# A selective-scan network on one core: two sums over states made a step later, their bank copied behind a decay, and two tiles for squares

## The chip, the core and the metric

The kernel runs on one core of a Trainium2 chip. The metric is the device time of one execution in microseconds (us). Engines are named as in the profile: PE (TensorE, matmuls), DVE (VectorE), ACT (ScalarE), POOL (GpSimd), SP (the queue that issues the DMAs).

## The reference, cut to what matters

Four images of 64 x 64 pixels and 96 channels pass four layers. Layer 0 normalises by groups, projects to 192 channels, convolves, and runs a selective scan along the rows and along the columns of the image, each of them forwards and backwards; then a depthwise and pointwise convolution (layer 1), attention without softmax and a quantised feed-forward network (layer 2), and a filter in the Fourier domain and a second feed-forward network (layer 3). The scan is the core of it:

```
def step(h, inp):
    u_t, dt_t, B_t, C_t = inp
    dA = jnp.exp(dt_t[..., None] * A)
    h = dA * h + (dt_t * u_t)[..., None] * B_t[:, None, :]
    y = jnp.sum(h * C_t[:, None, :], axis=-1)
    return (h, y)
...
def _ln_t(v, eps=1e-5):
    m = jnp.mean(v, axis=-1, keepdims=True)
    s = jnp.var(v, axis=-1, keepdims=True)
    return (v - m) / jnp.sqrt(s + eps)
```

There are 4 images x 2 orientations x 192 channels x 16 states x 4096 positions, each scanned in both directions. `y` is the sum over the 16 states of the state `h` times `C`.

## The kernel before, in words

A group is 8 channels with 16 states each, 128 rows, in one image and one orientation: N = 192 groups, numbered n. A group's 4096 positions are four chunks q = 0 to 3 of 1024. The loop over n (L1712) has eight steps a group, written out by hand: four forward (L1716, q rising) and four backward (L1764, k = 0 to 3, q falling). The order in which instructions are issued in the text is the order in each engine's queue.

In a step DVE runs one scan (L1741 forward, into a tile S; L1792 backward, in place in the decay's PSUM tile) and, backward, adds the result to S (L1802). From group 54 or so, when the other images' inputs have been made ("pre" in `done`), the last backward scan is left apart in a tile dl and not added. ACT computes the decays `pa` (`decay`, L1495), a step ahead, into two PSUM tiles of two banks each that take turns; so a decay waits for the scan that frees its tile. POOL multiplies by B before the scan (`times_b`, L1478) and by C after it (`times_c`, L1482, and `times_c_apart`, L1487). PE sums over states (`reduce`, L1509): a chunk is two matmuls with `red`, each into 32 rows of one PSUM bank, `py`; the profile counts a matmul of f32 as two instructions. Two chunks fill the bank, half 1 (chunks 3 and 2) or half 0 (chunks 1 and 0); `result` (L1517) copies the bank out to `ys` on ACT, and `store_result` issues four stores on SP. There is one bank `py`, so the next half's first sum waits for the copy of the last.

Before the change the order is, for group n:

- backward k = 1, 2, 3: products with C of chunks 3, 2, 1;
- backward k = 3: sums of chunks 3 and 2 (half 1);
- forward q = 0 of group n+1, at the end of the step: copy of half 1; the decay of chunk 2 comes next on ACT;
- q = 1: product of chunk 0 and sum of chunk 1; q = 2: the apart product, and the store of half 1;
- backward k = 0 of group n+1: sum of chunk 0; k = 2: copy of half 0; k = 3: its store.

There are five S tiles (`place_of`). Group n+1's scans of chunks 1, 2 and 3 write the tiles that held group n's S of chunks 3, 2 and 1, so each waits until that chunk has been summed.

Around these steps `pieces(step)` (called once a step) issues side work in small portions: the projections, convolutions and gates of images 1 to 3 (until about group 54), the turns of scanned data, and layers 1 to 3 of images 0 to 2. Each portion has a planned cost per engine (PE, ACT, POOL, DVE, DMA), and a portion is issued when the step's credit for the engines (`gains`, `short_gains`) allows it. `yield NEXT` puts the rest off to the next step; `clock[0]` counts steps. Side work has three PSUM banks (`bank_taker`); `held` is a list of evictions that wait their turn, with the step from which they count, and `settle` makes those with a cost on ACT wait one step more in the steps where ACT is short (residues 7, 0, 1).

Two pieces of side work are touched. Layer 1 (`layer1`) makes nine matmuls (L861) a block of 512 pixels and evicts them on ACT (`finish`, L833). The normalisation (`layernorm`) takes, for each block, a matmul that centres it (L905), two ACT instructions that copy it out (L894) and square it (L897), and a matmul that sums the squares into `p_var` (L887); it is split in two halves of four blocks. While the scan runs (`deep` = 1) a half has one tile for squares, so the square of a block waits for the variance matmul of the block before.

The part after the scan (from 5401 us) ends the side work and does image 3's layers 1 to 3 with all engines.

Of the kernel before, what the change touches and what calls it, by code (L numbers as in the profile page):

```python
# [19 lines left out]
HW = 64  # L20
L = HW * HW
C = 96
# [51 lines left out]
def layers(ctx: ExitStack, tc: tile.TileContext, a: dict, out):  # L74
# [137 lines left out]
    def settle(held):  # L212


        while held:
            cost, f, args, since = held[0]
            if cost[1]:
                while ordered[0] and clock[0] == since and (clock[0] - 1) % 8 in (7, 0, 1):
                    yield NEXT
            yield cost  # L220
            held.pop(0)
            f(*args)
# [580 lines left out]
    def rest(b, take, deep, x1t=None, held=None):  # L803
# [9 lines left out]
        def layer1(wk):  # L813
            x3 = (x1[b] if x1t is None else x1t).rearrange("p (r w) -> p r w", w=HW)

            def load(i):
                r0, lo, hi = rows_of(i)
                if x1t is not None:
                    return x3[:, lo:hi, :], clock[0]
                x = wk.tile([C, RPB + 2, HW], F32, tag="x", name="x", bufs=2)  # L820
                nc.sync.dma_start(x[:, : hi - lo, :], x3[:, lo:hi, :])
                return x, clock[0]

            def arrived(i):
                return done.get(("x1", b), 0) >= min(i + 2, NBLK)

            yield from until(lambda: arrived(0))
            nxt = load(0)
            yield NEXT
            held = []  # L830

            def finish(i, p, give):
                nc.scalar.activation(  # L833
                    t[:, blk(i)], p, AF.Identity, scale=l1s[:, 0:1], bias=l1s[:, 1:2]
                )
                give()
                ready["t1"] = i + 1

            for i in range(NBLK):
                r0, lo, hi = rows_of(i)  # L840
                if nxt is None:
                    yield NEXT
                    yield from settle(held)
                    yield from until(lambda: arrived(i))
                    nxt = load(i)
                    yield NEXT
                (x, since), nxt = nxt, None
                if clock[0] < since + LANDING:
                    yield NEXT
                    yield from settle(held)  # L850
                    yield from steps_past(since, LANDING)
                p, give = yield from take("p_l1", C, held=held)
                p3 = p.rearrange("p (r w) -> p r w", w=HW)
                for k, (ky, kx) in enumerate(conv_taps()):
                    if k % 3 == 0:
                        yield (2.4, 0, 0, 0, 0 if k else 1)
                        if nxt is None and i + 1 < NBLK and arrived(i + 1):
                            nxt = load(i + 1)
                    dy, dx, ra, rb, ca_, cb_ = tap_window(ky, kx, r0)
                    at = r0 + dy - lo  # L860
                    nc.tensor.matmul(  # L861
                        p3[:, ra:rb, ca_:cb_], lhsT=taps[:, ky * 3 + kx, :],
                        rhs=x[:, at + ra : at + rb, ca_ + dx : cb_ + dx],
                        start=(k == 0), stop=(k == 8),
                    )
                    if k == 2:
                        yield from settle(held)
                held.append(((0, 0.68, 0, 0), finish, (i, p, give), clock[0]))
            yield NEXT
            yield from settle(held)  # L870

        def layernorm(wk, hold, dst, source, result, previous=None):
# [3 lines left out]
            def half_of(h):  # L876
# [12 lines left out]
                def centred(i, pm, give):  # L889
                    if squares and deep == 1:  # L890
                        variance()
                    sq = wk.tile([C, BLK], F32, tag=f"sq{h}", name="sq", bufs=1 if deep == 1 else 4)
                    if ordered[0]:
                        nc.scalar.copy(hold[:, blk(i)], pm)  # L894
                    else:
                        nc.vector.tensor_copy(hold[:, blk(i)], pm)
                    nc.scalar.activation(sq, pm, AF.Square)  # L897
                    give()
                    squares.append((i, sq))
# [575 lines left out]
    def times_b(n, q):  # L1475

        if n < N:
            nc.gpsimd.tensor_tensor(Bs[n, q], Bs[n, q], reps[n // NG, 0, q], ALU.mult)  # L1478
# [19 lines left out]
    def reduce(n, half, chunks=(0, 1)):  # L1498

        if n < 0:  # L1500
            return
        if (n, half) not in pys:
            pys[n, half] = ps.tile([128, BLK], F32, tag="py", name="py")
        py = pys[n, half]
        for j in (2 * c + k for c in chunks for k in range(2)):
            q, k = 2 * half + j // 2, j % 2
            terms = [Ss[n, q]] + ([dls[n, 0]] if q == 0 and n in apart else [])
            for i, x in enumerate(terms):
                nc.tensor.matmul(  # L1509
                    py[32 * j : 32 * j + 32, :], lhsT=red, rhs=x[:, k * BLK : (k + 1) * BLK],  # L1510
                    start=(i == 0), stop=(i == len(terms) - 1),
                )
# [196 lines left out]
    with tc.manual_schedule():  # L1709
        ordered[0] = True  # L1710
        pas = [decay(0, 0, True), None, None, None]
        for n in range(N + 1):  # L1712
# [3 lines left out]
            for q in range(NCH):  # L1716

                if q < 2:
                    load_du(n + 1, q + 2)
                else:  # L1720
                    load_delta(n + 1, q - 2)
                if n % NG == 0 and 0 < n < N and q > 0:
                    load_rep(h, 1, 4 - q)
                if q < 3:
                    pas[q + 1] = decay(n, q + 1, q == 1)
                if q == 0:
                    times_b(n, 3)
                elif q == 1:
                    times_c(n - 1, 0)
                    reduce(n - 1, 0, (1,))  # L1730
                elif q == 2:
                    times_c_apart(n - 1)
                    store_result(n - 1, 1)
                else:
                    times_b(n + 1, 0)
                if end:
                    if q == 0:
                        result(n - 1, 1)
                    continue
                s = Ss[n, q] = big.tile([128, CH], F32, tag=f"S{place_of(n, q)}", name="S")  # L1740
                nc.vector.tensor_tensor_scan(  # L1741
                    s, pas[q], Bs[n, q], Ss[n, q - 1][:, CH - 1 : CH] if q else 0.0,
                    ALU.mult, ALU.add,
                )
                pieces(q)
                if q == 0:
                    result(n - 1, 1)
            if end:
                reduce(n - 1, 0, (0,))
                result(n - 1, 0)  # L1750
# [13 lines left out]
            for k, q in enumerate(reversed(range(NCH))):  # L1764
                if k < 2:
                    times_b(n + 1, k + 1)
                if k > 0:
                    times_c(n, q + 1)
                if k == 0:
                    reduce(n - 1, 0, (0,))  # L1770
                elif k == 1:
                    load_du(n + 2, 0)
                    load_delta(n + 1, 2)
                elif k == 2:
                    load_delta(n + 1, 3)
                else:
                    store_result(n - 1, 0)
                    load_du(n + 2, 1)
                if n % NG == NG - 2:
                    load_rep(h + 1, 0, k)  # L1780
                if k == 1:
                    pas[1] = decay(n, 1, False)
                elif k == 2:
                    pas[0] = decay(n, 0, True)
                    result(n - 1, 0)
                elif k == 3:
                    first = decay(n + 1, 0, True)


                alone = k == 3 and "pre" in done  # L1790
                to = dls[n, 0] if alone else pas[q]
                nc.vector.tensor_tensor_scan(  # L1792
                    to[:, ::-1], pas[q][:, ::-1], Bs[n, q][:, ::-1],
                    edge if k else 0.0, ALU.mult, ALU.add,
                )
                if k < 3:
                    edge = big.tile([128, 1], F32, tag="edge", name="edge", bufs=2)
                    nc.vector.tensor_copy(edge, to[:, 0:1])
                if alone:
                    apart.add(n)  # L1800
                else:
                    nc.vector.tensor_tensor(Ss[n, q], Ss[n, q], to, ALU.add)  # L1802
                if k == 3:
                    reduce(n, 1)
                pieces(4 + k)
                if n == N - 1:
                    for i in (2 * k, 2 * k + 1):
                        last_loads(last_place, i)
# [129 lines left out]
```

## Time and profile before

| what | value |
|---|---|
| median of the runs (3) | 5851.89 us (5849.64 to 5853.17) |
| the profiled execution's own time | 5842.19 us |
| its span | 5840.4 us |
| mean granted PE clock | 0.775 |
| first and last scan | 347 and about 5400 us |

The page gives each engine's busy time with its share of the span, and for each line of the kernel the number of instructions, their busy time, the mean of one in ns, and how long the engine was idle just before them, with what ended most of that. In "A <- B" the first is the instruction that waited, the second what released it.

### The profile page before, as it was taken

What the parts mean: (1) busy time and instruction counts of PE and PEld (TensorE: products, weight loads), DVE (VectorE), ACT (ScalarE), POOL (GpSimd) and SP (SyncE); (2) the same over time, 40 slices, a digit from 0 to 9 for tenths busy, and PEclk for the clock granted to TensorE, in tenths of its full rate; (3) what the DMA queues carried; (4) which work ended last, traced back from release to release, by engine and by line L of the source; (5) the groups of instructions that cost most, each with busy time, mean ns of one, the idle gap of its engine ahead of it and who ended that gap; (6) DMA issues with size and microseconds to landing.
All of it is one profiled execution on the core that took longest, in us unless ns stands there. A gap on an engine that the chain in (4) does not pass through costs nothing. (4 is left out here: it accounts for less than half of the span.)

```text
span 5840.4 us, 64640 instructions
## 1 busy us (share of the span) xinstructions
PE 4230.1 (72%) x19658; PEld 1612.3 (28%) x19658; DVE 4797.6 (82%) x3478; ACT 3044.6 (52%) x4205; POOL 4416.6 (76%) x2151
## 2 busy tenths in 40 slices
PE   8978888878973776664566776667678667667888
PEld 3322222222210221241331121245222114323345
DVE  2058898888899898998799999999999999979364
ACT  4667766766563346545454446444444554434233
POOL 1268888888889788888778989888898898867200
PEclk9979888888876776676777876668678767777888
DMA  3258878876698888788988867679887578886013
GB/s 105 80 163 233 234 215 225 242 221 195 187 253 237 222 216 223 206 243 237 246 240 224 228 185 211 194 212 249 230 235 206 164 210 235 245 230 191 22 39 104
DMA packets 469673, 1173.30 MB, mean 201 GB/s; under 512 B 90720, under 2 KB 155852, under 8 KB 469196
## 3 DMA queue, kind: packets, MB, share of 16 engines
q1 hardware_dynamic: 469324, 1169.17, 73.1%
q8 instruction: 156, 2.56, 0.2%
q14 instruction: 193, 1.58, 0.1%
HBM read 1012.05 MB, written 156.76 MB: 200 GB/s over the span
## 5 line engine op out<-in xcount | busy, mean ns | idle before, releaser
L1482 POOL TENSOR_TENSOR S<-S,rep 128x1024 f32<-128x1024 f32 x768 | 1807.6, 2356 | 541.5 <-DVE S L1802 485.4
L1495 ACT ACTIVATE pa<-dl,nega 128x1024 f32<-128x1024 f32 x1152 | 1285.3, 1117 | 1441.8 <-DVE S L1802 1076.0
L1478 POOL TENSOR_TENSOR B<-B,rep 128x1024 f32<-128x1024 f32 x768 | 1798.6, 2357 | 128.6 <-DMA B<-du_s 76.7
L1741 DVE TENSOR_TENSOR_SCAN S<-pa,S,B 128x1024 f32<-128x1024 f32 x576 | 1352.1, 2347 | 316.2 <-ACT pa L1495 128.6
L1509 PE MATMUL py<-S,red 128*32 128x512 f32 x3072 | 905.5, 845 | 739.9 <-POOL S L1482 491.4
L1792 DVE TENSOR_TENSOR_SCAN pa<-pa,edge,B 128x1024 f32<-128x1024 f32 x438 | 1029.7, 2351 | 46.3 <-ACT pa L1495 46.2
L1802 DVE TENSOR_TENSOR S<-S,pa 128x1024 f32<-128x1024 f32 x630 | 763.3, 1212 | 1.9
L1741 DVE TENSOR_TENSOR_SCAN S<-pa,B 128x1024 f32<-128x1024 f32 x192 | 436.4, 2273 | 189.5 <-ACT pa L1495 179.3
L390 PE MATMUL p_conv<-low,conv_w 128*96 128x512 f32 x1152 | 569.2, 647 | 8.7 <-ACT u L402 5.4
L1509 PEld LDWEIGHTS py<-S,red 128*32 128x32 f32 x3072 | 110.0, 125 | 1227.5 <-POOL S L1482 694.0
L1792 DVE TENSOR_TENSOR_SCAN pa<-pa,B 128x1024 f32<-128x1024 f32 x192 | 440.8, 2296 | 5.4
L154 ACT COPY side<-side 96x256 f32<-96x256 f32 (+1 forms) x448 | 278.9, 629 | 177.9 <-DMA deltaT_s<-side 74.5
L390 PE MATMUL p_conv<-high,conv_w 128*96 128x512 f32 (+1 forms) x768 | 356.6, 602 | 0.0
L1792 DVE TENSOR_TENSOR_SCAN dl<-pa,edge,B 128x1024 f32<-128x1024 f32 x138 | 323.1, 2341 | 16.3 <-ACT pa L1495 16.3
L1487 POOL TENSOR_TENSOR dl<-dl,rep 128x1024 f32<-128x1024 f32 x138 | 325.7, 2360 | 0.1
L1083 POOL CAST h<-y 128x1536 fp8e5<-128x1536 f16 x64 | 95.6, 1493 | 303.9 <-ACT y L794 286.3
L390 PEld LDWEIGHTS p_conv<-low,conv_w 128*96 128x96 f32 x1152 | 198.4, 179 | 390.8 <-issue 364.0
L905 PE MATMUL p_mean<-t,centre 96*96 96x512 f32 x256 | 174.8, 795 | 97.6 <-ACT sq L897 45.0
L1509 PE MATMUL py<-dl,red 128*32 128x512 f32 x552 | 219.2, 715 | 22.4 <-POOL dl L1487 22.3
L555 PE MATMUL p_y<-side,ident 96*96 96x512 f32 x336 | 207.1, 764 | 37.0 <-DVE q L948 11.6
L1517 ACT COPY ys<-py 128x512 f32<-128x512 f32 x384 | 221.9, 578 | 19.6 <-PE py L1509 18.2
L861 PE MATMUL p_l<-x,taps 96*96 96x504 f32 (+3 forms) x432 | 205.7, 629 | 16.4 <-DMA x<-x 12.5
(224 smaller groups left out, 5741.0 us busy)
## 6 DMA issues: line engine op xcount, KB each, us to landing
B<-du_s SPq DMA_DIRECT2D x768, 256.0 KB
dl<-delta_s SPq DMA_DIRECT2D x768, 256.0 KB
B<-duT_s SPq DMA_DIRECT2D x768, 256.0 KB
dl<-deltaT_s SPq DMA_DIRECT2D x768, 256.0 KB
z_s<-z SPq DMA_DIRECT2D x48, 512.0 KB
zl<-z_s SPq DMA_DIRECT2D x64, 384.0 KB
side<-y_s SPq DMA_DIRECT2D x120, 192.0 KB
rep<-bc_s SPq DMA_DIRECT2D x64, 256.0 KB
```

The costliest lines, as they stand in the source:

```text
L154: nc.scalar.copy(o.rearrange("p (w h) -> p w h", h=HW), t[:n, :].rearrange("p (h w) -> p w h", w=HW)[:, q * w : (q + 1) * w, :],)
L390: nc.tensor.matmul(p, lhsT=conv_w[: src.shape[0], k, oc * C : (oc + 1) * C], rhs=src[:, ky : ky + RPB, kx : kx + HW], start=(k == 0), stop ...
L555: nc.tensor.matmul(p, lhsT=ident[:C, :C], rhs=x, start=(j == 0), stop=(j == 2))
L1478: nc.gpsimd.tensor_tensor(Bs[n, q], Bs[n, q], reps[n // NG, 0, q], ALU.mult)
L1482: nc.gpsimd.tensor_tensor(Ss[n, q], Ss[n, q], reps[n // NG, 1, q], ALU.mult)
L1487: nc.gpsimd.tensor_tensor(dls[n, 0], dls[n, 0], reps[n // NG, 1, 0], ALU.mult)
L1495: nc.scalar.activation(pa, dls[n, q], AF.Exp, scale=nega[:, g : g + 1])
L1509: nc.tensor.matmul(py[32 * j : 32 * j + 32, :], lhsT=red, rhs=x[:, k * BLK : (k + 1) * BLK], start=(i == 0), stop=(i == len(terms) - 1),)
L1517: nc.scalar.copy(ys, pys.pop((n, half)))
L1741: nc.vector.tensor_tensor_scan(s, pas[q], Bs[n, q], Ss[n, q - 1][:, CH - 1 : CH] if q else 0.0, ALU.mult, ALU.add,)
L1792: nc.vector.tensor_tensor_scan(to[:, ::-1], pas[q][:, ::-1], Bs[n, q][:, ::-1], edge if k else 0.0, ALU.mult, ALU.add,)
L1802: nc.vector.tensor_tensor(Ss[n, q], Ss[n, q], to, ALU.add)
```

## The change

- The sum of chunk 2 moves from backward k = 3 to forward q = 0 of the next group; chunk 3's stays. So L1509 sums one chunk at a time in all four places.
- The copy of half 1 moves from the end of q = 0 to q = 1, behind the decay of chunk 2 on ACT.
- The sum of chunk 1 moves from q = 1 to q = 2, behind that copy (it writes the same bank).
- `layernorm` gets two tiles for squares per half while the scan runs (four after it, as before). For the space, layer 1's input tile x shares the buffers of the feed-forward network's tile `y16`, which is used later.
- Layer 1's eviction counts from the next step on: it is issued at least one step after its matmuls, in the steps with residues 7, 0, 1 two. `settle` is written so that this is possible; for other evictions it does what it did.

```diff
@@ settle
-                while ordered[0] and clock[0] == since and (clock[0] - 1) % 8 in (7, 0, 1):
+                while ordered[0] and clock[0] < since + ((clock[0] - 1) % 8 in (7, 0, 1)):
                     yield NEXT
@@ layer1
-                x = wk.tile([C, RPB + 2, HW], F32, tag="x", name="x", bufs=2)
+
+                x = wk.tile([C, RPB + 2, HW], F32, tag="y16", name="x", bufs=2)
...
-                held.append(((0, 0.68, 0, 0), finish, (i, p, give), clock[0]))
+                held.append(((0, 0.68, 0, 0), finish, (i, p, give), clock[0] + 1))
@@ layernorm
-                    sq = wk.tile([C, BLK], F32, tag=f"sq{h}", name="sq", bufs=1 if deep == 1 else 4)
+                    sq = wk.tile([C, BLK], F32, tag=f"sq{h}", name="sq", bufs=2 * deep)
@@ forward steps
                 if q == 0:
                     times_b(n, 3)
+                    reduce(n - 1, 1, (0,))
                 elif q == 1:
                     times_c(n - 1, 0)
-                    reduce(n - 1, 0, (1,))
+                    result(n - 1, 1)
                 elif q == 2:
                     times_c_apart(n - 1)
+                    reduce(n - 1, 0, (1,))
                     store_result(n - 1, 1)
                 else:
                     times_b(n + 1, 0)
                 if end:
-                    if q == 0:
-                        result(n - 1, 1)
                     continue
...
                 pieces(q)
-                if q == 0:
-                    result(n - 1, 1)
@@ backward steps
                 if k == 3:
-                    reduce(n, 1)
+                    reduce(n, 1, (1,))
                 pieces(4 + k)
```

## The prediction

> **What bounds the kernel now.** I read the page first, for which engine is full and which line idles it. One line each for the busy times and for the sums over states:
>
> ```profile
> PE 4230.1 (72%) x19658; PEld 1612.3 (28%) x19658; DVE 4797.6 (82%) x3478; ACT 3044.6 (52%) x4205; POOL 4416.6 (76%) x2151
> L1509 PE MATMUL py<-S,red 128*32 128x512 f32 x3072 | 905.5, 845 | 739.9 <-POOL S L1482 491.4
> ```
>
> VectorE (DVE) is fullest, and the sums are where TensorE (PE) idles most: 491.4 us for GpSimd's products. What counts is what of this reaches DVE. The windows (stretch, its length, busy us of each engine, granted clock, DMA) cut the scan part, 347 to 5401 us, in eights of 24 groups; the two first and two later:
>
> ```profile
> 347.00:996.00 649.00, 533.69 (x1306) 162.02 (x1306) 563.82 (x360) 446.42 (x632) 550.97 (x292) 0.86 0.79 221
> 996.00:1649.00 653.00, 543.92 (x1282) 159.04 (x1283) 564.60 (x362) 427.99 (x592) 557.21 (x290) 0.83 0.77 215
> 2269.00:2900.00 631.00, 357.23 (x2601) 167.87 (x2597) 560.77 (x374) 331.02 (x465) 530.58 (x239) 0.68 0.85 233
> 2900.00:3527.00 627.00, 447.38 (x1718) 152.87 (x1719) 573.21 (x399) 302.12 (x405) 527.14 (x245) 0.77 0.82 219
> ```
>
> Over the eight, DVE is busy 4557 of 5054 us, so some 497 us of idling is all that this change can win. Early (images 1 to 3 are projected and convolved, 54 groups) a group takes 27.1 us and PE is busy 82%; later 26 us and 57 to 73%. The waits of PE in the early (348 to 1800 us) and late window (1800 to 5401), then ScalarE's (ACT) over the scan part (total us, times, longest):
>
> ```profile
> PE py L1509 <- POOL S L1482: 105.4, 20, 13.1
> PE py L1509 <- ACT ys L1517: 38.0, 9, 9.4
> ```
> ```profile
> PE py L1509 <- POOL S L1482: 386.0, 98, 12.5
> PE py L1509 <- ACT ys L1517: 102.2, 35, 12.1
> ```
> ```profile
> ACT sq L897 <- PE p_var L887: 75.2, 43, 8.3
> ACT t L833 <- PE p_l L861: 67.1, 19, 8.8
> ACT ys L1517 <- PE py L1509: 18.2, 10, 2.8
> ```
>
> So PE's waits at the sums are mostly late, where it has time; ACT waits little for the sums but 75.2 us for the variance. I then followed each DVE idle time over 0.33 us back: its releaser, that engine's last idle time, its releaser, three times. Late: 32.5 us (17 places) lead to a square that waited for a variance matmul, 12.9 (9) to the joint sum of chunks 3 and 2 waiting for GpSimd, 13.4 (8) to chunk 1's sum waiting for the copy of the bank, 5.5 (2) to layer 1's eviction, 124 to DMAs. Early: 61 to PE's other work, 61 to DMAs, 13 to an S tile that a sum still reads. Last, an early group's timeline, PE and then DVE (start, us, idle before):
>
> ```profile
> 1599.83 1.07 PE L1509 MATMUL py<-S,red 128*32 128x512 f32 x8
> 1600.82 2.82 PE L390 MATMUL p_conv<-low,conv_w 128*96 128x512 f32 x6
> 1603.47 2.74 PE L390 MATMUL p_conv<-high,conv_w 128*96 128x512 f32 x6
> 1606.14 1.05 PE L1509 MATMUL py<-S,red 128*32 128x512 f32 x4
> 1607.12 2.38 PE L390 MATMUL p_conv<-high,conv_w 64*96 64x512 f32 x5
> ```
> ```profile
> 1601.11 2.35 DVE L1741 TENSOR_TENSOR_SCAN S<-pa,S,B 128x1024 f32<-128x1024 f32 x1 [2.43 <-PE py L1509]
> 1603.65 2.35 DVE L1741 TENSOR_TENSOR_SCAN S<-pa,S,B 128x1024 f32<-128x1024 f32 x1 [0.19 <-DVE S L1741]
> 1607.40 2.35 DVE L1741 TENSOR_TENSOR_SCAN S<-pa,S,B 128x1024 f32<-128x1024 f32 x1 [1.39 <-PE py L1509]
> ```
>
> PE runs without a gap, and DVE waits for it twice: the scan of chunk 1 writes the tile that held S of chunk 3 of the group before, the scan of chunk 3 that of chunk 1. The last starts 0.2 us after chunk 1's sum ends (1606.14 + 1.05 = 1607.19).
>
> **What the Trainium skill says.** *TensorE: Matmul & The Clock Gate*, "Architectural detail": matmuls stay in program order and ACT and DVE are strict FIFOs. The timeline agrees: convolutions stand behind the sum. Same page, "What's actually happening": PE is at half clock when it has been idle, at full when busy. The sum of one chunk takes 1.05 us here and 1.93 at 4001 us elsewhere (there for two chunks). *TensorEngine Tiling (Array Packing)*, "Key Properties": column strips run beside each other; here the four strips of two chunks took 1.07 us, the two of one chunk 1.05, so a chunk that is summed apart costs a full sum. *Perfetto Trace Analysis*, "Matmuls": independent groups should rotate through PSUM banks. The sums have one, py, and PE's 38.0 + 102.2 us for ys are its price.
>
> **The change, part by part.**
> (1) *Two tiles for squares.* No instruction more; the square of a block no longer waits for the variance of the block before. Of the 32.5 us I take 22 back; bounds 5 (the bank of p_mean is late next) and 32.
> (2) *Chunk 2's sum a step later.* At the last backward step PE now sums chunk 3 alone, whose product GpSimd made two steps before, and the side work behind it starts at once. I take 10 of the 12.9 us; bounds 0 and 20, since waits below 0.33 us and deeper chains are not in it. Cost: 192 more sums of one chunk, 0.98 us of PE each at full clock (1606.14 to 1607.12), about 1.9 at half: 190 to 370 us on PE. Late, the 386 us of waits that go cover it. Early, they are 105.4 us in 54 groups, in 20 places, and where PE has no gap nothing covers it.
> (3) *Bank copied behind the decay.* The copy (0.58 us) leaves ACT's path to decay (n,2) and lies on the path to decay (n,3), which has the slack of a scan, 2.35 us, less its own 1.12. ACT waited 18.2 us at it. I take 4; bounds -5 and 14. Queued behind the copy on ACT are that step's evictions; SP's store of the copied rows comes a step later in its queue anyway, behind a load that waits for the same decay, so nothing for the queue.
> (4) *Chunk 1's sum a step later.* It waits for that copy, so its 13.4 us are moved, not removed: I take 3. What it adds: the scan of chunk 3 comes one step after it now, no longer two. I measured the time from the sum's end to that scan. Late, 4 of 137 are below 1 us and 28 below 2.5. Early, 16 of 54 are 0.2 us (released by it), 21 below 1, 41 below 2.5, median 1.5. How far does the sum move? By a step's side work on PE: (533.7 + 543.9 us busy less 184.2 in sums)/48 = 18.6 us a group; this step has 2.0 of the 23.2 PE credits, 1.6 us; with (2)'s 1.0 to 1.4 some 2.8 us. If nothing came back, 16 x 2.6 + 5 x 2.1 + 20 x 1.05 = 73 us early. But a DVE that stalls there lets a lagging PE catch up, and the 2.43 us stall of the timeline's first scan then goes; a PE-bound group pays only its added sum, 16 x 1 = 16 us. I take 20; bounds 0 and 73. Late I take 2; bounds 0 and 25.
> (5) *Layer 1's eviction a step later*: of 5.5 us I take 3. Loads set the pace of its blocks (four steps), so its end slips by a step at most. The x tile in y16's buffers frees the space; x is dead by the time y16 is written: nothing, at most a few us per image.
>
> Sum: -22 - 10 - 4 - 3 - 3 + 20 + 2 = -20 us. The profiled execution took 5842.2 (span 5840.4), which would give 5822; the median of the runs shown, 5851.9, lies 10 above, so **5832 us**.
>
> **The rivals.**
> A, the forecast: 5832, own range 5790 to 5840. For it: 58.8 us of late waits are named, and the early PE is no worse off in sum, since its waits at sums, 143 us, exceed the 54 added sums.
> B, slower: chunk 1's sum becomes the early bound. Nothing comes back (+73), and late gains shrink to 28: 5851.9 + 73 - 28 = **5897**. It decides where PE, at the end of a forward scan of chunk 2, is still in the side work ahead of that sum. For it: the 16 scans already released by the sum. Against it: PE's busy share is 82%, not 95%, and lag that DVE waits out is not waited out again.
> C, no change: the gains are 25 and the early cost as large, or (3) does nothing because late decays are late by DMA: **5852**, within 12 us.
>
> **How the numbers follow.** A 0.47, B 0.39, C 0.14. A measurement of this kernel tells about 0.2% (12 us) from no change; A is all faster, B slower, C the same. Range: A's low end with all bounds is about 5785 (a tenth of the chance lies below A's middle band); up to 5910 takes in B with some of (4)'s late bound. About 1 in 10 is left out on each side.
>
> **What would show it.** PE's wait for S L1482 falls from 491 to under 150 us; ACT's wait of sq for p_var from 75 to under 20; L1509 is in fours only. DVE idles less after 1800 us, by some 35 to 45. Wrong: scans at L1741 wait early for PE py by far more than the 13.5 us of now, groups before 1800 us take over 28 us, or the late idle time stays.

## The result, and the profile after

The change makes the kernel slower: 5901.3 us (median of 5 runs, 5889.9 to 5917.3) against 5852.6 us (5849.6 to 5859.6) measured beside it, a ratio of 1.0085 with an interval of 1.0065 to 1.0106. The forecast was 5832 us and faster; rival B's 5897 us lies within 5 us of the measured time. The profiled execution took 5917.3 us (span 5915.5, clock 0.782), 75 us more than the profiled one of before (span 5840.4). It is the slowest of its five runs, and the one of before lies 10 us under its median, so the two profiles show 75 us where the medians differ by 49; the parts read from them below are, taken together, too large by that difference. Lines from L820 on have moved by one: the sum is L1510, the copy of the bank L1518, the forward scan L1742, the product with C L1483.

First the page of the changed kernel: busy times, then the scans and the sums (busy us, mean ns, idle time before them and what ended most of it).

```profile
PE 4356.6 (74%) x19658; PEld 1633.6 (28%) x19658; DVE 4796.5 (81%) x3478; ACT 3048.5 (52%) x4205; POOL 4417.5 (75%) x2151
...
L1742 DVE TENSOR_TENSOR_SCAN S<-pa,S,B 128x1024 f32<-128x1024 f32 x576 | 1352.2, 2348 | 399.7 <-PE py L1510 128.7
L1510 PE MATMUL py<-S,red 128*32 128x512 f32 x3072 | 1063.8, 804 | 670.3 <-ACT ys L1518 524.8
```

The line of the scans on the page of before, which the prediction did not show:

```profile
L1741 DVE TENSOR_TENSOR_SCAN S<-pa,S,B 128x1024 f32<-128x1024 f32 x576 | 1352.1, 2347 | 316.2 <-ACT pa L1495 128.6
```

DVE does the same work in the same time (4796.5 against 4797.6 us), so the 75 us are idle time of DVE. At the scans it grew by 83 us, and what ended most of it is no longer a decay but a sum. The idle time before the sums fell by 70 us only: GpSimd's products, 491.4 us before, are no longer what ends most of it, but the copy of the bank is, with 524.8 us.

The windows over the same groups as in the prediction (24 each; stretch, length, busy us of PE, its weight loads, DVE, ACT, POOL, granted clock, DMA share, GB/s):

```profile
347.00:1009.00 662.00, 552.05 (x1309) 162.65 (x1310) 563.23 (x360) 447.48 (x631) 550.75 (x292) 0.87 0.78 216
1009.00:1690.00 681.00, 562.72 (x1276) 159.86 (x1274) 563.20 (x361) 428.32 (x591) 556.28 (x289) 0.83 0.74 207
2318.00:2954.00 636.00, 366.15 (x2604) 172.73 (x2596) 561.87 (x375) 332.39 (x466) 531.88 (x239) 0.67 0.85 231
2954.00:3576.00 622.00, 464.73 (x1721) 155.35 (x1721) 573.29 (x400) 302.59 (x405) 527.72 (x245) 0.79 0.83 220
```

The first stretch became 13 us longer, the second 28 (28.4 us a group), and PE's busy time there grew by 18 to 19 us, some 0.8 us a group. The third is 5 longer, the fourth 5 shorter.

PE's waits at the sums, early (347 to 1850 us) and then late (1850 to 5480 us): total us, times, longest.

```profile
PE py L1510 <- ACT ys L1518: 141.0, 24, 12.5
```
```profile
PE py L1510 <- ACT ys L1518: 383.8, 95, 12.2
```

DVE's waits for a sum at the forward scan, early and then late. In the kernel before they are 13.5 us early, as the prediction has it, and 14.8 us in the whole scan part.

```profile
DVE S L1742 <- PE py L1510: 74.8, 29, 5.1
```
```profile
DVE S L1742 <- PE py L1510: 53.8, 30, 10.0
```

Some 114 us of such waits were added. Part of it is not new time: a scan that stands gives ACT time, and the waits of scans for a decay fell from 307.9 to 248.8 us (some 165 us of each is one wait ahead of the first scan).

ACT's waits over the scan part: the square's wait for `p_var`, 75.2 us before, is down to 3.8 us; the two others are

```profile
ACT ys L1518 <- PE py L1510: 64.7, 36, 5.2
...
ACT t L834 <- PE p_l L862: 57.1, 17, 8.2
```

The timeline of the same group as in the prediction (group 46's forward steps), PE and then DVE (start, us, idle before):

```profile
1637.79 1.05 PE L1510 MATMUL py<-S,red 128*32 128x512 f32 x4
1638.78 2.82 PE L390 MATMUL p_conv<-low,conv_w 128*96 128x512 f32 x6
1641.52 1.05 PE L1510 MATMUL py<-S,red 128*32 128x512 f32 x4
1642.51 5.56 PE L390 MATMUL p_conv<-high,conv_w 128*96 128x512 f32 x12
1647.99 1.05 PE L1510 MATMUL py<-S,red 128*32 128x512 f32 x4
```
```profile
1639.05 2.35 DVE L1742 TENSOR_TENSOR_SCAN S<-pa,S,B 128x1024 f32<-128x1024 f32 x1 [2.40 <-PE py L1510]
1642.77 2.35 DVE L1742 TENSOR_TENSOR_SCAN S<-pa,S,B 128x1024 f32<-128x1024 f32 x1 [1.38 <-PE py L1510]
1649.25 2.35 DVE L1742 TENSOR_TENSOR_SCAN S<-pa,S,B 128x1024 f32<-128x1024 f32 x1 [4.12 <-PE py L1510]
```

All three scans start 0.2 us after a sum's end (chunks 3, 2, 1 of the group before). PE has no gap: between the sums it does convolutions, 2.8 and 5.6 us. Before, DVE waited at two of the three, 3.8 us in all; now at three, 7.9 us. Over all 192 groups I counted the scans that start within 0.3 us of the end of the sum that frees their tile. Chunk 3's, released by chunk 1's sum: 16 before, all in the first 48 groups, with 20 us of idle time; 60 after, with 122 us, of which 29 with 74 us lie in the first 48. Chunk 2's, released by chunk 2's sum: none before, 19 with 26 us after.

And a place late in the scan part, which no line of before has. PE, then DVE:

```profile
2040.66 1.05 PE L1510 MATMUL py<-S,red 128*32 128x512 f32 x4
2041.81 1.07 PE L582 MATMUL p_out<-side,w_out 96*96 96x512 f32 x2
2042.81 1.05 PE L1510 MATMUL py<-S,red 128*32 128x512 f32 x4
2052.89 7.28 PE L862 MATMUL p_l<-x,taps 96*96 96x512 f32 x12 [9.03 <-DMA x<-x]
2060.09 1.05 PE L1510 MATMUL py<-S,red 128*32 128x512 f32 x4
```
```profile
2048.98 2.35 DVE L1742 TENSOR_TENSOR_SCAN S<-pa,S,B 128x1024 f32<-128x1024 f32 x1 [0.30 <-DVE S L1742]
2061.35 2.35 DVE L1742 TENSOR_TENSOR_SCAN S<-pa,S,B 128x1024 f32<-128x1024 f32 x1 [10.02 <-PE py L1510]
```

PE has plenty of time here, but layer 1's matmuls of step q = 1 wait 9.03 us for a load, and chunk 1's sum, which stood ahead of them before, now stands behind them in PE's program order. DVE waits 10.02 us for a sum of 1.05 us.

For the experiments I cut each profiled execution in three: early (from the first scan, at 342 to 348 us, to the first scan of group 54), late (to the end of the last scan) and the rest. Each ratio is to the kernel before, measured beside it. The parts are of one execution each, and whole executions of one kernel spread by up to 30 us (the 23 of before beside "sums only" took 5819 to 5849 us), so a part is good to about 10 us (an estimate).

| kernel | ratio to before (95%) | early us | late us | rest us |
|---|---|---|---|---|
| before | 1 | 1451 | 3593 | 449 |
| the change | 1.0085 (1.0065 to 1.0106) | 1494 | 3621 | 453 |
| sums only | 1.0126 (1.0109 to 1.0143) | 1494 | 3619 | 448 |
| all but the sums ("the rest alone") | 0.9951 (0.9934 to 0.9967) | 1458 | 3560 | 448 |
| squares only | 0.9948 (0.9931 to 0.9965) | 1451 | 3566 | 446 |
| change, chunk 1's sum back | 1.0050 (1.0036 to 1.0064) | 1473 | 3605 | 444 |
| change, sixth S tile | 0.9995 (0.9985 to 1.0005) | 1454 | 3566 | 453 |
| change, one ys (control) | 1.0130 (1.0112 to 1.0148) | 1497 | 3629 | 457 |
| all but the sums, sixth tile | 0.9995 (0.9985 to 1.0004) | 1453 | 3593 | 456 |
| chunk 2's sum apart, nothing else of the sums | 1.0040 (1.0024 to 1.0056) | 1484 | 3589 | 443 |
| copy and chunk 1 later, no split | 1.0045 (1.0028 to 1.0063) | 1473 | 3605 | 450 |
| change, copy of half 0 earlier | 1.0055 (1.0037 to 1.0072) | 1482 | 3600 | 443 |
| all but the sums, chunk 1 earlier | 1.0012 (1.0004 to 1.0019) | 1449 | 3603 | 451 |
| all but the sums, chunk 3 summed twice | 1.0003 (0.9993 to 1.0013) | 1473 | 3578 | 449 |

### The profile page after: what moved, and what is told of

It is laid out like the page before. It is cut to its first block, busy times and chain, and to the rows that moved or that the text cites. A ratio compares the mean times of both kernels' runs of the same rounds, so it can differ in the third digit from the quotient of the medians.

```text
span 5915.5 us, 64867 instructions
## 1 busy us (share of the span) xinstructions
PE 4356.6 (74%) x19658; PEld 1633.6 (28%) x19658; DVE 4796.5 (81%) x3478; ACT 3048.5 (52%) x4205; POOL 4417.5 (75%) x2151
## 5 line engine op out<-in xcount | busy, mean ns | idle before, releaser
L1483 POOL TENSOR_TENSOR S<-S,rep 128x1024 f32<-128x1024 f32 x768 | 1807.9, 2356 | 618.7 <-DVE S L1801 569.7
L1742 DVE TENSOR_TENSOR_SCAN S<-pa,S,B 128x1024 f32<-128x1024 f32 x576 | 1352.2, 2348 | 399.7 <-PE py L1510 128.7
L1510 PE MATMUL py<-S,red 128*32 128x512 f32 x3072 | 1063.8, 804 | 670.3 <-ACT ys L1518 524.8
L1742 DVE TENSOR_TENSOR_SCAN S<-pa,B 128x1024 f32<-128x1024 f32 x192 | 436.4, 2273 | 188.3 <-ACT pa L1496 174.3
L1510 PEld LDWEIGHTS py<-S,red 128*32 128x32 f32 x3072 | 136.6, 122 | 1228.7 <-issue 936.7
L1518 ACT COPY ys<-py 128x512 f32<-128x512 f32 x384 | 222.8, 580 | 78.6 <-PE py L1510 64.7
L1510 PE MATMUL py<-dl,red 128*32 128x512 f32 x552 | 211.7, 694 | 23.2 <-POOL dl L1488 23.1
```

Source lines behind the costliest of these rows:

```text
L1483: nc.gpsimd.tensor_tensor(Ss[n, q], Ss[n, q], reps[n // NG, 1, q], ALU.mult)
L1510: nc.tensor.matmul(py[32 * j : 32 * j + 32, :], lhsT=red, rhs=x[:, k * BLK : (k + 1) * BLK], start=(i == 0), stop=(i == len(terms) - 1),)
L1518: nc.scalar.copy(ys, pys.pop((n, half)))
L1742: nc.vector.tensor_tensor_scan(s, pas[q], Bs[n, q], Ss[n, q - 1][:, CH - 1 : CH] if q else 0.0, ALU.mult, ALU.add,)
```

## The experiments

The theory (S in the expectations): the loss comes by the five S tiles. The sums now reach PE later, behind more side work, and the scans that write the same tiles wait for them. The rivals: PE's new load alone costs the time, wherever it stands (L); or the wait for the bank's copy does; or the parts that are not the sums do (R).

**Which half of the change loses.** Two kernels split it: the moves at the sums alone, and all the rest (two tiles for squares, x in y16's buffers, layer 1's eviction).

```diff
@@ sums only: the change without these three
-sq = wk.tile([C, BLK], F32, tag=f"sq{h}", name="sq", bufs=2 * deep)
+sq = wk.tile([C, BLK], F32, tag=f"sq{h}", name="sq", bufs=1 if deep == 1 else 4)
-x = wk.tile([C, RPB + 2, HW], F32, tag="y16", name="x", bufs=2)
+x = wk.tile([C, RPB + 2, HW], F32, tag="x", name="x", bufs=2)
-held.append(((0, 0.68, 0, 0), finish, (i, p, give), clock[0] + 1))
+held.append(((0, 0.68, 0, 0), finish, (i, p, give), clock[0]))
```

> The kernel before with only the moves at the sums (chunk 2 a step later, bank copied behind the decay, chunk 1 a step later); one tile for squares, layer 1 as before. Theory S (the scan of chunk 3 waits for the tile that chunk 1's sum, now a step later, still reads) and theory L (the 192 extra sums load TensorE): all of the loss is here, 5895 to 5930 us, and the scan line waits for PE py by over 100 us. Theory R (the other parts of the change cost): 5850 to 5865 us.

> The kernel before with only the other parts: two tiles for squares, layer 1's eviction a step later, x in y16's buffers; the sums as before. Theories S and L: no loss, a small gain from the squares, 5820 to 5850 us, ACT's wait of sq for p_var under 10 us. Theory R: 5885 to 5905 us.

Measured: the sums alone 1.0126, the rest alone 0.9951. The loss is all in the moves at the sums, 1.3%, and the rest wins 0.5%. The rest alone is faster than both kernels. In its trace the square waits 9.9 us for the variance, and PE waits for GpSimd's products as before:

```profile
PE py L1510 <- POOL S L1483: 499.6, 121, 13.5
PE py L1510 <- ACT ys L1518: 146.9, 45, 12.7
```

**Which part of the rest wins.** The rest without layer 1's later eviction:

```diff
-held.append(((0, 0.68, 0, 0), finish, (i, p, give), clock[0] + 1))
+held.append(((0, 0.68, 0, 0), finish, (i, p, give), clock[0]))
```

> The kernel before with the two tiles for squares (and x in y16's buffers) alone. The run with squares and layer 1 was 0.995. If the squares carry the gain: 0.994 to 0.997, ACT's wait of sq for p_var under 12 us. If layer 1's later eviction carries it: 0.998 to 1.001.

Measured 0.9948, the same as with it. The second tile for squares carries the whole gain, 0.5% or 30 us, all of it late (3593 to 3566 us); layer 1's eviction is worth nothing that can be told.

**Is it chunk 1's place?** The change with its sum back at q = 1, right behind the copy:

```diff
                     result(n - 1, 1)
+                    reduce(n - 1, 0, (1,))
                 elif q == 2:
                     times_c_apart(n - 1)
-                    reduce(n - 1, 0, (1,))
```

> The changed kernel with chunk 1's sum back in step q = 1, right behind the copy of the bank and ahead of that step's side work; chunk 2's sum stays apart and late, the copy stays behind the decay. Theory S: most of the loss goes, 5840 to 5865 us; scans released by chunk 1's sum before 1850 us fall from 35 to under 20. Theory L: the number of sums is unchanged, so 5885 to 5905 us stay.

Measured 1.0050: 0.35% comes back, in both parts of the scan. In the first 48 groups the scans released by chunk 1's sum fall from 29 to 17, and all waits of scans for sums fall from 128.7 to 52.4 us, as theory S has it; but 1.0% over the rest alone stays, and the 5868 us lie between the two forecasts. The sum now waits for the copy at the head of a step, with that step's side work behind it: PE's waits for the copy are 636.2 us (165 times) against 525 in the change. That this wait costs what stays is argued and not shown. So where chunk 1's sum stands is a part of the loss, not the whole.

**Is it the S tile?** A sixth tile, so that the scan of chunk 2 writes a tile that was summed one step earlier than now (chunk 3's), that of chunk 3 one summed two steps earlier (chunk 2's), and that of chunk 1 a tile long free. The space for it comes from `ys` and `stats` with one buffer each instead of two. That costs something by itself, so the control has it with five tiles.

```diff
@@ sixth tile, in place_of
-        return (4, 3, 2, 1)[q] if n % 2 else q
+        return (4, 5, 3, 2)[q] if n % 2 else q
@@ sixth tile and control
-tag="ys", name="ys", bufs=2)
+tag="ys", name="ys", bufs=1)
-tag="stats", name="stats", bufs=2)
+tag="stats", name="stats", bufs=1)
```

> The changed kernel with a sixth tile for S, so that the scan of chunk 3 writes the tile of chunk 2 of the group before (summed two steps earlier) and not of chunk 1; for the space ys and stats have one buffer. Theory S: the wait for the tile is gone, DVE's wait at the scan for PE py under 50 us in all, 5825 to 5860 us. Theory L: TensorE has the same sums, the wait goes to evictions and decays, 5885 to 5905 us.

> The changed kernel with one buffer for ys and for stats and five S tiles: the control for the run with six tiles, which needed that space. Theory S: ScalarE's copies wait for the stores as they did there (some 130 us), but the tile wait is back: 1.008 to 1.015 of the kernel before, so the sixth tile alone is worth 0.9 to 1.5%. If the gain there came from another cause (a shift of the stores): 0.999 to 1.003 here too.

Measured 0.9995 with six tiles and 1.0130 in the control: the sixth tile is worth 1.35%. DVE's waits for sums and PE's for the copy, of the kernel with six tiles:

```profile
DVE S L1742 <- PE py L1510: 1.5, 5, 0.4
```
```profile
PE py L1510 <- ACT ys L1518: 551.6, 126, 12.7
```

and of the control:

```profile
DVE S L1742 <- PE py L1510: 172.7, 75, 8.9
```
```profile
PE py L1510 <- ACT ys L1518: 567.1, 126, 12.9
```

PE waits for the copy as long in both (551.6 and 567.1 us), and it does the same sums in both. What differs is that DVE waits 1.5 us for the sums in one and 172.7 in the other. So neither PE's load nor its wait for the bank makes this 1.35% by itself; they cost it only where a scan waits behind a sum.

**Do the two orders differ at all with six tiles?** The same two edits on the rest alone:

> Squares and layer 1 as in the change, sums and copies as in the kernel before, with a sixth S tile (one buffer for ys and stats, which cost about 0.45% in the changed kernel). Theory S: here the tile waits are some 30 us in the kernel before, so at most 0.5% comes back, which the ys buffer eats: 0.992 to 0.999 of the kernel before. If it is under 0.990 the tile held up more than the waits at the scan show.

Measured 0.9995, as the change with six tiles. With five tiles and two `ys` buffers the two orders are 1.34% apart (0.9951 and 1.0085), with six tiles and one 0.00%. Hence most of the loss of the moves at the sums passes through the S tiles. That all of it does is not shown, since the single `ys` buffer need not cost the same in both orders. In the change it costs 0.45% (1.0085 to 1.0130); the old order with one `ys` buffer and five tiles was not run. There the copy stands ahead of a decay and waits longer for the stores of its only buffer, 198.4 us against 127.1 in the change with six tiles, and the scans' waits for decays are 359.3 us against 292.8 in the rest alone:

```profile
ACT ys L1518 <- DMA yT_s<-ys: 106.9, 34, 7.8
ACT ys L1518 <- DMA y_s<-ys: 91.5, 23, 12.8
```

If this longer wait eats a gain from the 18.1 us of waits for a tile that the rest alone has, up to 0.3 of the 1.34% lies outside the tiles (an estimate from these numbers).

**The moves one by one.** First only chunk 2's sum apart and a step later, on the rest alone, with the copy at the end of q = 0 and chunk 1 at q = 1 as before; then only the copy behind the decay and chunk 1 a step later, with chunks 3 and 2 in one sum.

```diff
@@ split only (on the rest alone)
                     times_b(n, 3)
+                    reduce(n - 1, 1, (0,))
...
-                    reduce(n, 1)
+                    reduce(n, 1, (1,))
@@ later, no split (on the change)
                     times_b(n, 3)
-                    reduce(n - 1, 1, (0,))
...
-                    reduce(n, 1, (1,))
+                    reduce(n, 1)
```

> Squares and layer 1 as in the change, and of the sums only chunk 2's moved (summed apart, a step later); the bank's copy and chunk 1's sum stay in their old places. Against the run without any move at the sums (0.995 of the kernel before). Theory L (192 more sums on TensorE): most of the 1.3% of loss is here, 1.003 to 1.008. Theory S: a small part, 0.995 to 1.000, as chunk 1's sum is a step ahead of its scan as before.

> Squares and layer 1 as in the change, the copy behind the decay and chunk 1's sum a step later, but chunks 3 and 2 summed together in the last backward step as before (no more sums than before). Theory S: most of the loss is here, 1.002 to 1.008, and scans released by chunk 1's sum stay over 25 early. Theory L: no loss, 0.993 to 0.998.

Measured 1.0040 and 1.0045, so each alone costs 0.9% over the rest alone, and both together 1.34%, less than their sum. For the split alone this is what theory L forecast, not S; for the later copy it is S, not L. They lose in different places. With the split alone the copy stands ahead of the decay of chunk 2 on ACT and waits for a sum that now comes later:

```profile
ACT ys L1518 <- PE py L1510: 164.0, 73, 10.8
```

while the scans wait for sums 20.1 us only. They wait for decays instead, 57 us more than in the rest alone (292.8 us), so this loss does not come by an S tile:

```profile
DVE S L1743 <- ACT pa L1496: 350.2, 125, 164.0
```

With the later copy and chunk 1 alone it is the scans, as in the change, and the split is not needed for it:

```profile
DVE S L1741 <- PE py L1510: 102.5, 54, 6.0
```

In the first 48 groups chunk 1's sum releases 23 scans of chunk 3 there, with the same 74 us of idle time as in the change. From there the split adds 0.40% (1.0045 to 1.0085).

**What does PE's load cost by itself?** The rest alone, with chunk 3 summed a second time at the last backward step. The second sum writes the same values to the same place, so 192 sums of one chunk are added and none is moved.

```diff
                     reduce(n, 1)
+                    reduce(n, 1, (1,))
```

> Squares and layer 1 as in the change, sums and copies in the places of the kernel before, but chunk 3 is summed twice in the last backward step (the second overwrites the first with the same values): the change's TensorE load, 192 sums more, without its moves. Theory S: little, 0.995 to 1.000. Theory L: 1.001 to 1.006.

Measured 1.0003, between the two forecasts: 0.52% over the rest alone, early 15 us and late 18. The sums' busy time grew by 208 us (917.8 to 1125.8), and the scans' waits for sums from 18.1 to 43.4 us. So the rival of the load is right in part: in the old order the load alone costs 0.52%, and it too makes scans wait longer for sums. That is close to the 0.40% that the split adds above. Taken in this order, load or split is 0.4 to 0.5% of the loss, and the other 0.9% is the later place of the copy and of chunk 1's sum; taken in the other order the split alone costs 0.9%, by the copy ahead of the decay, so the shares are not fixed.

**Is the bank's wait the cause late?** The change, with the copy of half 0 one step earlier (backward k = 1, behind the decay of chunk 1), so that chunk 3's sum finds the bank free:

```diff
@@ decays of the backward steps
                     pas[0] = decay(n, 0, True)
-                    result(n - 1, 0)
...
                     pas[1] = decay(n, 1, False)
+                    result(n - 1, 0)
```

> The changed kernel with the copy of half 0 a step earlier (backward k = 1, behind the decay of chunk 1), so that chunk 3's sum need not wait for the bank. Theory: TensorE's wait at the sums for the copies (525 us in the changed kernel) falls below 300, but the time stays within 1.005 to 1.012 of the kernel before, because that wait stood before work that nothing on VectorE waited for. If the bank wait costs time: under 1.003.

Measured 1.0055, 0.30% better than the change, at the edge of what the intervals tell apart. The wait for the copy halves, and a wait for the products takes its place:

```profile
PE py L1510 <- POOL S L1483: 296.9, 90, 9.6
PE py L1510 <- ACT ys L1518: 241.5, 69, 8.8
```

The two make 538 us, against some 548 in the change (525 and 23), and the scans wait for sums 117.2 us, against 128.7. The bank's wait is at most a small part of the loss, and PE waits about as long for whichever comes last.

**The other direction.** On the rest alone, the copy of half 1 and chunk 1's sum ahead of the side work of q = 0, a step earlier than before the change:

```diff
                     times_b(n, 3)
+                    result(n - 1, 1)
+                    reduce(n - 1, 0, (1,))
                 elif q == 1:
                     times_c(n - 1, 0)
-                    reduce(n - 1, 0, (1,))
```

> The opposite move: squares and layer 1 as in the change, chunks 3 and 2 summed together as before, but the copy of half 1 and chunk 1's sum before the side work of q = 0, a step earlier than in the kernel before. Theory S: scans of chunk 3 released by chunk 1's sum go to none, early idle before that scan falls from 0.9 us a group to about 0.5; against it the copy stands ahead of side evictions and of the decay of chunk 2 and waits there when TensorE lags: 0.988 to 1.000, likeliest 0.993. If the copy's wait wins: over 1.000.

Measured 1.0012, 0.6% worse than the rest alone: a miss. Early it is as good as squares only (1449 against 1451 us), but late it loses what the squares had won (3603 against 3566). PE's waits for the copy grew from 146.9 to 256.1 us and the copy's for the sum from 19.6 to 30.9. The copy is ahead of the decay again, as with the split alone, but the scans' late waits for decays are only 88.8 us against 81.6, of some 41 us more that DVE idles late. The largest single growth is of scans that wait for a load of B, from 7.6 to 19.8 us; the cause of the late loss stays open.

## Why the prediction was wrong, step by step

Its sum of −20 us was +20 early and −40 late; the medians differ by +49. The profiled executions differ by +43 early, +27 late and +4 after the scan. Two steps failed: that the waits which go cover the added sums late (2), and that chunk 1's sum, made a step later, costs 2 us late and 20 early because PE catches up while DVE stalls (4).

- **(1) Squares: right.** Forecast −22 us, bounds −5 and −32; squares only measured −0.52%, 30 us, and the trace has it late, as said. The test (75.2 to under 20 us) held, with 3.8.
- **(5) Layer 1: nothing** where −3 was taken. ACT's wait for its matmuls fell from 67.1 to 57.1 us only, and the time did not.
- **(3) The copy behind the decay: not shown as a gain.** Its waits grew from 18.2 to 64.7 us, since the sum that it waits for comes later. Behind the decay they cost less than ahead of it (164.0 us of waits in the split alone). With the copy there, chunk 1's sum cannot be at q = 1 without a wait (1.0050).
- **(2) Chunk 2's sum: failed, late.** The step said that the 386 us of late waits "that go" cover the added sums. The waits for the products went, but 383.8 us for the bank's copy stand in their place: 241.2 ahead of chunk 3's sum, which waits for the copy of half 0, and 142.6 ahead of chunk 1's, which waits for that of half 1. Nor did the waits cover the load where they stayed: with chunk 3 summed twice PE waits 528.8 us for the products, and the added sums still cost 0.52%, 18 us of it late. PE's slack in the late stage is real, but it lies ahead of these sums, not between them and their scans. A wait absorbs only what is queued ahead of it.
- **(4) Chunk 1's sum: failed, and the largest miss.** Two terms of it. Late I took 2 us, bounds 0 and 25: I had counted how near the scan came to the old sum, not what waits in the side work that now lies ahead of it. There a load reaches DVE (9.03 us of waiting from 2043 us on), or 8.14 us of layer 1's matmuls (at 4492 us, ahead of a scan that waits 9.74 us). Late, the moves at the sums cost 26 us (sums only against before) to 55 (the change against squares only), where (2) to (4) had −15. The 55 is some 20 too large, since with 43 early it would exceed the 1.34%, 78 us, of the ratios. Early I took 20 with the reason that "a DVE that stalls there lets a lagging PE catch up": the moves cost 43 us, about twice that and some 60% of the bound of 73. In the timeline shown the reason does not hold: after a stall of 2.40 us the next two scans stall again, for 1.38 and 4.12 us, because PE has side work of its own between each pair of sums and no gap to catch up in.

The tests on record went so: the wait for the products fell (to 23 us) as in the forecast, and each chunk is summed by itself, but scans wait early for sums 74.8 us instead of 13.5, groups of the second stretch take 28.4 us, and the late idle time grew. The first two tests thus told nothing of the time.

**Rival B** was right in sign and, for the early part, in mechanism. Its parts were not right in size: early +73 and late −28 were forecast, +43 and +27 found. That its total is so near is luck, because the errors cancel.

What I argued and did not show: why the split and the later copy add up to less than their sum, how the late loss divides between loads, clock and side work ahead of the sum, and how much of it would be left with a spare tile at no price in `ys`.

## What to carry to other kernels

A matmul that frees a buffer is as urgent as the writer that waits for the buffer, however idle its engine is on average. Before moving it later past side work on an in-order queue, count how many steps its buffer has to spare, and what can wait in that side work, loads included. A wait that is named is not a gain: ask what is late next, and whether anything of the bounding engine stood behind the wait at all. When several edits come together, cost them against the one resource they share; here the squares alone (0.9948) were the whole gain.

## What the runs showed of the hardware

- The added sums were cheaper on PE than estimated: 192 more of them took 158 us (905.5 to 1063.8), 0.82 us each instead of 0.98 to 1.9, and the mean instruction fell from 845 to 804 ns. In *TensorE: Matmul & The Clock Gate*, "What's actually happening", the Trainium skill says that PE is at half clock after idling and at full when busy; the traces agree: in the changed kernel a sum of one chunk takes 1.05 us in the busy stretch at 1638 us, where the granted clock was 1.00 (1634 to 1640 us), and 1.92 us at 4486 us, where it was 0.50 (4486 to 4488). Where the second, repeated sum was added with no move, it cost 1.08 us on average.
- PE's idle time at the sums says nothing on the time of this kernel. It is 739.9 us before and 670.3 in the slower change; and with six tiles it is 746.4 us in the new order and 902.1 in the old one, at the same ratio of 0.9995.
